# Seven block products for eight in the two dense layers of layer 3 of a graph network

## The chip, the cores and the metric

The kernel runs on one core of a Trainium2 chip. The metric is the device time of one execution in microseconds, as the median of several runs.

## The reference

32 graphs (B) of 512 nodes (N) with 256 features (D) pass through four layers. Each layer multiplies a full adjacency matrix with the features, passes the result through dense layers, adds the layer's input and normalizes each row (a layer norm over 256 features). All is f32.

```python
# x: (32, 512, 256), adj: (32, 512, 512)
x = ln(x + relu(((1 + eps0) * x + adj @ x) @ W1_0 + b1_0) @ W2_0 + b2_0)     # layer 0, hidden 512
h = adj @ (x @ W.T + b);  x = ln(x + where(h > 0, h, alpha * h))               # layer 1
h = ln(x) * gamma + beta
x = ln(x + x + relu(adj @ h @ W_rel + b_rel + h @ W_root))                     # layer 2
agg = eps3 * x + adj @ x                                                       # layer 3, hidden 1024
h = silu(rmsnorm(agg @ W1_3 + b1_3) * w_3)
x = ln(x + h @ W2_3 + b2_3)
```

## The kernel before

**One graph.** `adjT` holds the transposed adjacency matrix as four row blocks of 128 x 512 (8 KB a partition in all). The self loops are written into its diagonal blocks by GpSimd (POOL): `dg` saves the old diagonal, `loop0` and `loop3` are added for layers 0 and 3, and `rows` is the sum over the four blocks, whose column sums are needed in layers 1 and 2. `aggregate` multiplies `x` with `adjT` (four products of 512 columns into one PSUM bank, for each half j of the features), and ScalarE (ACT) copies the bank to `aT`, features on partitions. `dense_feat` keeps features on partitions (512 columns, two banks at a time), `dense_tok` gives tokens on partitions (256 columns). `Norm` computes a layer norm: VectorE (DVE) takes statistics of each block of 128 tokens (`half`), POOL takes the power -0.5 (`inv_sqrt`, tile `rstd`), DVE scales the four blocks (`scaled`).

**Layer 3**, where the change is, in `graph`: dense 1 is `dense_feat(aT, W1_3, f0)`, eight feature tiles of 128 x 512, two at a time. DVE adds the bias and writes `hT` (tile by tile), ACT squares the same bank (`acc`, `sq`), POOL adds the squares up in `acc`. `column_sums(acc)` (products with `ones`, one column each) gives the sum of squares of each token; DVE makes `ve` of it (L375), POOL the power, and four transposes against `ident` (L380) spread 1/rms over the partitions. DVE multiplies the eight tiles of `hT` with it (L385), ACT applies Silu (L386). Dense 2 is `dense_tok([(hT, W2_3)], h)` for two halves of the tokens, DVE adds `xb` (the layer's input and bias) into `r`, and the last `Norm` gives the output.

In layer 1 the product with W_1 is followed by a chain on DVE and ACT: `v`, `neg`, `s`, `r`, then a norm with two powers at once (128 x 8) that gives both the input of layer 2 (`h` in the change, `x` before) and a scaled copy (`xx`). `u` is the bias of layer 2, made from `rs` (the column sums of `rows`).

**The order.** Two graphs are under way at a time (STREAMS = 2): the generator `graph` yields after each piece of PE work, with a number of PE columns for which the stream is not to be resumed. Only PE's order is set by hand in this way: at each step the stream of the lowest graph number whose time has come goes on, and where none is due the count jumps ahead. `columns` counts what PE has been given, by a cost for each product. The order on DVE, ACT, POOL and the DMA queue comes from a scheduler at build time; each engine then takes its own queue strictly in that order.

```python
    WAIT_COPY, WAIT_NORM, WAIT_NORM2 = 2000, 11000, 17000
    WAIT_SQUARES, WAIT_RMS, WAIT_SILU = 6000, 5000, 8000
            columns[0] = max(columns[0], min(s[1] for s in live))
            s = min(s for s in live if s[1] <= columns[0])
```

**Buffers.** The pool `work` has two buffers for each name, shared by both streams (`v` and `neg` have one), `load` has three for `x` and `adjT`, PSUM eight banks. `prepare` loads a graph two graphs ahead; it is called in layer 3 (`successor`). Before the first graph, `fold_norm` multiplies gamma and beta of layer 2 into W_rel and W_root; these are PE's first products.

Of the kernel before, what the change touches and what calls it, by code (L numbers as in the profile page):

```python
# [12 lines left out]
P = 128  # L13
# [5 lines left out]
def tile_gnn_stack(ctx: ExitStack, tc: tile.TileContext, a: dict, out: bass.AP):  # L19
# [10 lines left out]

    nc = tc.nc
# [7 lines left out]
    HC = NC // 2  # L39

    const = ctx.enter_context(tc.tile_pool(name="const", bufs=1))
    load = ctx.enter_context(tc.tile_pool(name="load", bufs=3))
    work = ctx.enter_context(tc.tile_pool(name="work", bufs=2))
# [77 lines left out]
    def mm(o, lhsT, rhs, start, stop):  # L121
        nc.tensor.matmul(o, lhsT, rhs, start=start, stop=stop)  # L122
        columns[0] += 4 * max(o.shape[-1], P // 2)
# [15 lines left out]
    def tok(name, **kw):  # L139
        return work.tile([P, NC, D], F32, tag=name, name=name, **kw)  # L140

    def feat(name, n=DC, **kw):
        return work.tile([P, n, N], F32, tag=name, name=name, **kw)
# [40 lines left out]
    class Norm:  # L184
# [22 lines left out]
        def scaled(self, s, name):  # L207

            y = tok(name)
# [6 lines left out]

    def inv_sqrt(ve, name):
# [5 lines left out]
    def plus_row(x, r, name):  # L223

        y = tok(name)
        for h in range(2):
            nc.gpsimd.tensor_add(half(y, h), half(x, h), r.unsqueeze(1).to_broadcast([P, HC, D]))  # L227
        return y


    def load_graph(b):
        adjT = load.tile([P, NC, N], F32, tag="adjT", name="adjT")
# [5 lines left out]
    def prepare(b):  # L238

        x, adjT = load_graph(b)  # L240
        dg = work.tile([P, NC, P], F32, tag="dg", name="dg")
# [3 lines left out]
        rows = work.tile([P, N], F32, tag="rows", name="rows")  # L245
        nc.gpsimd.tensor_add(rows, adjT[:, 0, :], adjT[:, 1, :])
        for m in range(2, NC):
            nc.gpsimd.tensor_add(rows, rows, adjT[:, m, :])
        for m in range(NC):
            nc.gpsimd.tensor_add(loops[m], dg[:, m, :], loop0)  # L250
        return x, adjT, dg, rows, plus_row(x, b2_0, "xb")

    def graph(b, ready, successor):


        x, adjT, dg, rows, xb = ready
        loops = diagonal(adjT)


        aT = feat("aT")  # L260
# [5 lines left out]
        h1 = feat("h1", FC0)  # L266
# [5 lines left out]
        norm = Norm(tok("r"))  # L272
# [6 lines left out]
        x = norm.scaled(norm.scales((1.0, LN_EPS)), "x1")  # L279
# [3 lines left out]
        aT = feat("aT")  # L283
# [5 lines left out]
        u = tok("u")  # L289
        for c in range(NC):  # L290
            nc.vector.scalar_tensor_tensor(
                u[:, c, :], shift_rel, rs[:, c : c + 1], shift_2, op0=ALU.mult, op1=ALU.add
            )
        aggregate(aT, x, adjT, 1)
        yield WAIT_COPY
        v = tok("v", bufs=1)
        neg = tok("neg", bufs=1)
        s = tok("s")
        norm = Norm(tok("r"))
# [17 lines left out]
        h = norm.scaled(q[:, 0:NC], "x2")  # L317
# [153 lines left out]
```

## Time and profile before

| | |
|---|---|
| runs | 2737.19, 2737.64, 2738.63 us; median 2737.64 |
| profiled execution | 2741.19 us, of which the span of its instructions is 2739.3 |
| busy share of the span | PE 98%, PEld (weight loads) 60%, DVE 48%, POOL 35%, ACT 24% |
| granted TensorE clock, mean | 0.993 |
| DMA | 73.14 MB, mean 27 GB/s |

An f32 product that the code writes once is recorded as two PE instructions, a transpose as one. "f32 x1536" in a group is the number of recorded instructions. A line with an engine and "L122" is the helper `mm`, so products are told apart by the tiles' names: `ps<-aT,L_gnn_W` is a dense layer with features on partitions, `pst<-L_gnn_W,hT` is dense 2 of layer 3, `pst<-L_gnn_W,h` is W2_0 of layer 0, `pst<-L_gnn_W,aT` is W_1 of layer 1, `ps<-ones,acc` is the sum of squares, `ps<-ident,rstd` are the transposes of 1/rms. In a timeline a row has its start in us, its length, the engine, line and operation, its count and, in brackets, the idle time before it and who ended that. A row of windows has, after the stretch and its length, the busy time of each engine with its instructions, the granted clock, the DMA share and GB/s.

### The profile page before, as it was taken

What the parts mean: (1) busy time and instruction counts of PE and PEld (TensorE: products, weight loads), DVE (VectorE), ACT (ScalarE), POOL (GpSimd) and SP (SyncE); (2) the same over time, 40 slices, a digit from 0 to 9 for tenths busy, and PEclk for the clock granted to TensorE, in tenths of its full rate; (3) what the DMA queues carried; (4) which work ended last, traced back from release to release, by engine and by line L of the source; (5) the groups of instructions that cost most, each with busy time, mean ns of one, the idle gap of its engine ahead of it and who ended that gap; (6) DMA issues with size and microseconds to landing.
All of it is one profiled execution on the core that took longest, in us unless ns stands there. A gap on an engine that the chain in (4) does not pass through costs nothing.

```text
span 2739.3 us, 24444 instructions
## 1 busy us (share of the span) xinstructions
PE 2671.0 (98%) x9096; PEld 1651.8 (60%) x9096; DVE 1307.3 (48%) x3053; ACT 652.8 (24%) x1026; POOL 957.5 (35%) x1138
## 2 busy tenths in 40 slices
PE   6899999999999999999999999999999999999997
PEld 3556665666666666665666656666566666656664
DVE  2535544455454545535445444554545555444453
ACT  1222222212222122222222222222221222212221
POOL 4422434334333333433334343243433333333222
PEclk9999999999999999999999999999999999999998
DMA  4000000000000000000000000000000000000000
GB/s 150 16 31 16 24 31 24 31 16 31 31 16 31 31 22 25 16 31 31 31 16 24 31 24 31 16 24 31 24 31 16 31 31 16 31 24 8 8 8 8
DMA packets 17319, 73.14 MB, mean 27 GB/s; under 512 B 1969, under 2 KB 4273, under 8 KB 13105
## 3 DMA queue, kind: packets, MB, share of 16 engines
q1 hardware_dynamic: 13824, 67.12, 6.8%
q10 hardware_dynamic: 2928, 3.93, 0.4%
q8 instruction: 72, 1.18, 0.2%
q0 software_dynamic: 448, 0.54, 0.1%
q14 instruction: 47, 0.38, 0.0%
HBM read 54.80 MB, written 16.78 MB: 26 GB/s over the span
## 4 chain that ended last, share of the span: by engine, by line
PE 83%; POOL 8%; DVE 3%; issue 2%; ACT 2%; DMA 1%; POOLq 0%; ACTq 0%; DVEq 0%
PE ps L122 48%; PE pst L122 34%; POOL acc L371 7%; ACT sq L370 2%; PE ps L329 1%; DVE hT L365 1%; POOL rstd L220 1%; DMA L_gnn_W_rel<-in_L_gnn_W_rel_dram 1%; DVE st L194 1%; PE ps L380 1%; DVE r L343 0%; DVE s L342 0%; DVE x L211 0%; DVE mv L195 0%; DVE s L308 0%
## 5 line engine op out<-in xcount | busy, mean ns | idle before, releaser
L122 PE MATMUL ps<-adjT,x 128*128 128x512 f32 x2048 | 921.1, 598 | 19.3 <-DVE x L211 19.3
L122 PE MATMUL ps<-aT,L_gnn_W 128*128 128x512 f32 x1536 | 669.8, 592 | 0.0
L122 PEld LDWEIGHTS ps<-adjT,x 128*128 128x128 f32 x2048 | 385.0, 191 | 454.4 <-issue 411.5
L122 PEld LDWEIGHTS ps<-aT,L_gnn_W 128*128 128x128 f32 x1536 | 291.8, 190 | 367.4 <-issue 336.8
L153 ACT ACTIVATE aT<-ps 128x512 f32<-128x512 f32 x256 | 152.9, 597 | 1445.4 <-PE ps L122 1445.4
L122 PE MATMUL pst<-L_gnn_W,hT 128*128 128x256 f32 x2048 | 459.6, 384 | 3.1 <-ACT hT L386 3.1
L220 POOL TENSOR_TENSOR rstd<-ve,mhalf 128x4 f32<-128x4 f32 (+1 forms) x160 | 185.4, 1159 | 719.8 <-DVE ve L201 677.2
L122 PEld LDWEIGHTS pst<-L_gnn_W,hT 128*128 128x128 f32 x2048 | 387.2, 191 | 70.6 <-ACT hT L386 17.8
L371 POOL TENSOR_TENSOR acc<-acc,sq 128x512 f32<-128x512 f32 x224 | 283.3, 1265 | 368.5 <-ACT sq L370 360.8
L365 DVE TENSOR_SCALAR hT<-ps,L_gnn_b_c 128x512 f32<-128x512 f32 x256 | 192.2, 751 | 388.0 <-PE ps L122 374.2
L211 DVE TENSOR_SCALAR x<-r,mv,rstd 128x256 f32<-128x256 f32 x512 | 209.8, 473 | 189.8 <-POOL rstd L220 189.8
L122 PE MATMUL pst<-L_gnn_W,h 128*128 128x256 f32 x1024 | 232.4, 380 | 0.0
L227 POOL TENSOR_TENSOR xb<-x,L_gnn_b 128x512 f32<-128x512 f32 x128 | 163.4, 1292 | 165.7 <-DVE r L275 138.5
L122 PEld LDWEIGHTS pst<-L_gnn_W,h 128*128 128x128 f32 x1024 | 192.2, 190 | 31.7 <-issue 7.7
L370 ACT ACTIVATE sq<-ps,L_gnn_b_c 128x512 f32<-128x512 f32 x224 | 153.8, 687 | 205.2 <-DVE hT L365 108.4
L194 DVE BATCH_NORM_STATS2 st<-r 128x6 f32<-128x256 f32 x512 | 193.8, 415 | 5.5
L386 ACT ACTIVATE hT<-hT,L_gnn_rms_weight_c 128x512 f32<-128x512 f32 x256 | 162.7, 710 | 110.6 <-DVE hT L385 110.6
L385 DVE TENSOR_TENSOR hT<-hT,ps 128x512 f32<-128x512 f32 x256 | 157.4, 676 | 25.5 <-PE ps L380 25.5
L275 DVE TENSOR_TENSOR r<-pst,xb 128x512 f32<-128x512 f32 x64 | 43.9, 686 | 239.6 <-PE pst L122 239.6
L265 POOL COPY adjT<-dg 128x128 f32<-128x128 f32 x128 | 52.5, 410 | 273.7 <-PE ps L122 273.5
L342 DVE TENSOR_TENSOR s<-pst,u 128x512 f32<-128x512 f32 x64 | 44.3, 692 | 206.0 <-PE pst L122 206.0
L122 PE MATMUL pst<-L_gnn_W_root,h 128*128 128x256 f32 x512 | 131.4, 379 | 0.0
(65 smaller groups left out, 1768.0 us busy)
## 6 DMA issues: line engine op xcount, KB each, us to landing
adjT<-in_adj_dram SPq DMA_DIRECT2D x32, 1024.0 KB, 4.7
x<-in_x_dram SPq DMA_DIRECT2D x32, 512.0 KB, 3.4
out_dram<-x SPq DMA_DIRECT2D x32, 512.0 KB, 2.6
L_gnn_W<-in_L_gnn_W_dram ACTq DMA_DIRECT2D x2, 1024.0 KB, 14.8
L_gnn_W<-in_L_gnn_W_dram ACTq DMA_DIRECT2D x2, 512.0 KB, 12.5
L_gnn_b<-in_L_gnn_b_dram POOLq DMA_DIRECT2D x3, 128.0 KB, 8.2
L_gnn_W<-in_L_gnn_W_dram ACTq DMA_DIRECT2D x1, 256.0 KB, 19.9
L_gnn_W_rel<-in_L_gnn_W_rel_dram ACTq DMA_DIRECT2D x1, 256.0 KB, 20.1
```

What stands on the lines that cost most here:

```text
L122: nc.tensor.matmul(o, lhsT, rhs, start=start, stop=stop)
L153: nc.scalar.activation(aT[:, j, :], ps, AF.Copy)
L194: nc.vector.bn_stats(self.st[:, c, :], self.r[:, c, :])
L211: nc.vector.tensor_scalar(y[:, c, :], self.r[:, c, :], self.mv[:, c, 0:1], s[:, c : c + 1], op0=ALU.subtract, op1=ALU.mult,)
L220: nc.gpsimd.tensor_tensor(t, ve, mhalf[:, 0:n], op=ALU.pow)
L227: nc.gpsimd.tensor_add(half(y, h), half(x, h), r.unsqueeze(1).to_broadcast([P, HC, D]))
L265: nc.gpsimd.tensor_copy(loops[m], dg[:, m, :])
L365: nc.vector.tensor_scalar(hT[:, f, :], ps, bias, None, op0=ALU.add)
L370: nc.scalar.activation(sq, ps, AF.Square, bias=bias)
L371: nc.gpsimd.tensor_add(acc, acc, sq)
L385: nc.vector.tensor_mul(hT[:, f, :], hT[:, f, :], pr)
L386: nc.scalar.activation(hT[:, f, :], hT[:, f, :], AF.Silu, scale=w_3[:, f : f + 1])
```

## The change

Both dense layers of layer 3 are cut into 2 x 2 blocks on each side, and their product is formed by seven block products (Winograd's form of Strassen's method) where eight were needed. Four sums of blocks of each weight matrix are made once (`weight_sums`), four sums of blocks of the activations for each graph: dense 1 takes its sums of `aT` on DVE and POOL, dense 2 its sums of `hT` after the Silu, in part in place.

`seven` orders the products over three PSUM banks. Bank x takes m1, is read, and then goes on adding m6, m7 and m4, and is read after each; bank z takes m5, is read, and adds m3; bank y takes m2. So the partial sums of the method stay in PSUM. The first three reads (`take`) go to tiles `part`, the other four (`put`) make the blocks of the result. In dense 1 a product is two written matmuls of 256 columns (one step in K), and there are two rounds of seven; in dense 2 it is eight of 128 columns, one round. In dense 1 ACT now does the `take`s, half of the last `put` and the squares of two tiles at once, from SBUF; the last two additions to `acc` are on DVE.

Each stream has tiles of its own under a few names that several values share one after the other (`Slots`): `aT` and the norm's `r` share one, `x1`, `u` and the last `r` another, `h1`, `zT` and `hT` a third. `x` has two buffers for three. The sum `rows` moves from `prepare` into layer 0, `u` from layer 1 into layer 2, and the folding of gamma and beta into the first graph's layer 0. The cost per product in `mm` has another lower limit, WAIT_SQUARES is 9000 for 6000, and a WAIT_READ of 2000 stands ahead of m4.

```diff
+    TH = N // 2
+    STREAMS = 2
     const = ctx.enter_context(tc.tile_pool(name="const", bufs=1))
-    load = ctx.enter_context(tc.tile_pool(name="load", bufs=3))
-    work = ctx.enter_context(tc.tile_pool(name="work", bufs=2))
+    load = ctx.enter_context(tc.tile_pool(name="load", bufs=2))
+    work = ctx.enter_context(tc.tile_pool(name="work", bufs=1))
...
-    def mm(o, lhsT, rhs, start, stop):
-        nc.tensor.matmul(o, lhsT, rhs, start=start, stop=stop)
-        columns[0] += 4 * max(o.shape[-1], P // 2)
+    def mm(o, lhsT, rhs, start, stop, **kw):
+        nc.tensor.matmul(o, lhsT, rhs, start=start, stop=stop, **kw)
+        columns[0] += 4 * max(o.shape[-1], P + 4)
...
+        def tile(self, shape, tag, name):
+            return work.tile(shape, F32, tag=f"{tag}_{self.stream}", name=name)
...
+    def part():
+        return work.tile([P, 2, TH], F32, tag="part", name="part", bufs=6)
+    def scratch(name, **kw):
         return work.tile([P, NC, D], F32, tag=name, name=name, **kw)
...
+    def weight_sums(name, a11, a12, a21, a22):
+        t = const.tile([P, 4, *a11.shape[1:]], F32, tag=name, name=name)
+        s1, s2, s3, s4 = (t[:, i] for i in range(4))
+        nc.vector.tensor_add(s1, a21, a22)
+        nc.vector.tensor_sub(s2, s1, a11)
+        nc.vector.tensor_sub(s3, a11, a21)
+        nc.vector.tensor_sub(s4, a12, s2)
+        return dict(m1=a11, m2=a12, m3=s4, m4=a22, m5=s1, m6=s2, m7=s3)
...
+    def seven(product, quarter, take, put):
...
+        x, y, z = (psum.tile([P, *quarter], F32, tag="ps", name=n) for n in ("psx", "psy", "psz"))
+        product("m1", x, True)
+        t1 = take(x, 0, 0)
+        yield 0
+        product("m2", y, True)
+        put(y, t1, 0, 0)
+        product("m5", z, True)
+        t5 = take(z, 1, 1)
+        yield 0
+        product("m6", x, False)
+        t6 = take(x, 0, 1)
+        yield 0
+        product("m3", z, False)
+        put(z, t6, 0, 1)
+        yield 0
+        product("m7", x, False)
+        put(x, t5, 1, 1)
+        yield WAIT_READ
+        product("m4", x, False)
+        put(x, None, 1, 0)
...
     def load_graph(b):
-        adjT = load.tile([P, NC, N], F32, tag="adjT", name="adjT")
+        adjT = load.tile([P, NC, N], F32, tag="adjT", name="adjT", bufs=STREAMS + 1)
         x = load.tile([P, NC, D], F32, tag="x", name="x")
...
+        own = slots[b % STREAMS]
+        dg = own.tile([P, NC, P], "dg", "dg")
...
-        rows = work.tile([P, N], F32, tag="rows", name="rows")
-        nc.gpsimd.tensor_add(rows, adjT[:, 0, :], adjT[:, 1, :])
-        for m in range(2, NC):
-            nc.gpsimd.tensor_add(rows, rows, adjT[:, m, :])
         for m in range(NC):
             nc.gpsimd.tensor_add(loops[m], dg[:, m, :], loop0)
-        return x, adjT, dg, rows, plus_row(x, b2_0, "xb")
+        return x, adjT, dg, plus_row(own.tok("xb", "xb"), x, b2_0)
...
+        rows = own.tile([P, N], "rows", "rows")
+        nc.gpsimd.tensor_add(rows, adjT[:, 0, :], adjT[:, 1, :])
+        for m in range(2, NC):
+            nc.gpsimd.tensor_add(rows, rows, adjT[:, m, :])
+        h1 = own.feat("h", "h1", FC0)
...
-        norm = Norm(tok("r"))
+        if b == 0:
+            setup_weights()
+        norm = Norm(own.tok("aT", "r"))
...
-        u = tok("u")
-        for c in range(NC):
-            nc.vector.scalar_tensor_tensor(
-                u[:, c, :], shift_rel, rs[:, c : c + 1], shift_2, op0=ALU.mult, op1=ALU.add
-            )
...
-        v = tok("v", bufs=1)
-        neg = tok("neg", bufs=1)
-        s = tok("s")
-        norm = Norm(tok("r"))
+        v = scratch("v")
+        neg = scratch("neg")
+        s = scratch("s")
+        norm = Norm(own.tok("aT", "r"))
...
+        h = norm.scaled(q[:, 0:NC], own.tok("x2", "h"))
+        xx = norm.scaled(q[:, NC : 2 * NC], own.tok("xb", "xx"))
...
-        aT = feat("aT")
-        hT = feat("h1")
+        aT = own.feat("aT", "aT")
+        hT = own.feat("h", "zT")
+        u = own.tok("x1", "u")
+        for c in range(NC):
+            nc.vector.scalar_tensor_tensor(
+                u[:, c, :], shifts["rel"], rs[:, c : c + 1], shifts["2"], op0=ALU.mult, op1=ALU.add
+            )
...
-        t = tok("s")
-        norm = Norm(tok("r"))
+        t = scratch("s")
+        norm = Norm(own.tok("aT", "r"))
...
-        x = norm.scaled(norm.scales((1.0, LN_EPS)), "x1")
-        xb = plus_row(x, b2_3, "xb")
+        x = norm.scaled(norm.scales((1.0, LN_EPS)), own.tok("x1", "x1"))
+        xb = plus_row(own.tok("xb", "xb"), x, b2_3)
...
-        hT = feat("hT", FC3)
-        acc = work.tile([P, N], F32, tag="acc", name="acc")
-        for f0 in range(0, FC3, 2):
-            for i, ps in enumerate(dense_feat(aT, W1_3, f0)):
-                f = f0 + i
-                bias = b1_3[:, f : f + 1]
-                nc.vector.tensor_scalar(hT[:, f, :], ps, bias, None, op0=ALU.add)
-                if f == 0:
-                    nc.scalar.activation(acc, ps, AF.Square, bias=bias)
-                else:
-                    sq = work.tile([P, N], F32, tag="sq", name="sq", bufs=3)
-                    nc.scalar.activation(sq, ps, AF.Square, bias=bias)
-                    nc.gpsimd.tensor_add(acc, acc, sq)
-            yield WAIT_SQUARES if f0 + 2 == FC3 else 0
+        hT = own.feat("h", "hT", FC3)
+        acc = own.tile([P, N], "rows", "acc")
+        t = own.tile([P, 4, TH], "t", "t")
+        b11, b12, b21, b22 = (aT[:, k, j * TH : (j + 1) * TH] for k in range(2) for j in range(2))
+        t1, t2, t3, t4 = (t[:, i] for i in range(4))
+        nc.vector.tensor_sub(t1, b12, b11)
+        nc.vector.tensor_sub(t2, b22, t1)
+        nc.gpsimd.tensor_sub(t3, b22, b12)
+        nc.gpsimd.tensor_sub(t4, b21, t2)
+        right = dict(m1=b11, m2=b21, m3=b22, m4=t4, m5=t1, m6=t2, m7=t3)
+        FH = FC3 // 2
+        for f0 in range(0, FH, 2):
+            def product(m, ps, first):
+                for i in range(2):
+                    w = A1_3[m][:, (f0 + i) * P : (f0 + i + 1) * P]
+                    mm(ps[:, i, :], w, right[m], first and i == 0, True, skip_group_check=True)
+            def take(ps, i, j):
+                t = part()
+                nc.scalar.activation(t, ps, AF.Copy)
+                return t
+            def put(ps, t, i, j):
+                for n in range(2):
+                    f = i * FH + f0 + n
+                    o = hT[:, f, j * TH : (j + 1) * TH]
+                    bias = b1_3[:, f : f + 1]
+                    if t is None:
+                        nc.scalar.activation(o, ps[:, n, :], AF.Identity, bias=bias)
+                    else:
+                        nc.vector.scalar_tensor_tensor(
+                            o, ps[:, n, :], bias, t[:, n, :], op0=ALU.add, op1=ALU.add
+                        )
+                if i != j:
+                    f = i * FH + f0
+                    sq = work.tile([P, 2, N], F32, tag="sq", name="sq", bufs=2)
+                    nc.scalar.activation(sq, hT[:, f : f + 2, :], AF.Square)
+                    if f == 0:
+                        nc.gpsimd.tensor_add(acc, sq[:, 0, :], sq[:, 1, :])
+                    else:
+                        e = nc.vector if f + 2 == FC3 else nc.gpsimd
+                        e.tensor_add(acc, acc, sq[:, 0, :])
+                        e.tensor_add(acc, acc, sq[:, 1, :])
+            yield from seven(product, (2, TH), take, put)
+            yield WAIT_SQUARES if f0 + 2 == FH else 0
...
+        t1 = own.tile([P, FH, TH], "aT", "t1")
+        t2 = own.tile([P, FH, TH], "t", "t2")
+        b11, b12, b21, b22 = (
+            hT[:, k * FH : (k + 1) * FH, j * TH : (j + 1) * TH] for k in range(2) for j in range(2)
+        )
+        for q in (slice(0, FH // 2), slice(FH // 2, FH)):
+            nc.vector.tensor_sub(t1[:, q], b12[:, q], b11[:, q])
+        for q in (slice(0, FH // 2), slice(FH // 2, FH)):
+            nc.vector.tensor_sub(t2[:, q], b22[:, q], t1[:, q])
+            nc.gpsimd.tensor_sub(b12[:, q], b22[:, q], b12[:, q])
         yield WAIT_SILU
-        norm = Norm(tok("r"))
-        for h in range(2):
-            ps = dense_tok([(hT, W2_3)], h)
-            nc.vector.tensor_add(half(norm.r, h), ps, half(xb, h))
-            norm.half(h)
-            if h == 0:
-                yield 0
-        y = norm.scaled(norm.scales((1.0, LN_EPS)), "x2")
+        norm = Norm(own.tok("x1", "r"))
+        right = dict(m1=b11, m2=b21, m3=b22, m4=b21, m5=t1, m6=t2, m7=b12)
+        def product(m, ps, first):
+            for i in range(HC):
+                for k in range(FH):
+                    mm(
+                        ps[:, i, :], right[m][:, k, i * P : (i + 1) * P], A2_3[m][:, k, :],
+                        first and i == 0 and k == 0, k == FH - 1, skip_group_check=True,
+                    )
+            if m == "m2":
+                for q in (slice(0, FH // 2), slice(FH // 2, FH)):
+                    nc.gpsimd.tensor_sub(b21[:, q], b21[:, q], t2[:, q])
+        def block(t, i, j):
+            return t[:, j * HC : (j + 1) * HC, i * P : (i + 1) * P]
+        def take(ps, i, j):
+            t = part()[:, :, 0:P]
+            nc.vector.tensor_add(t, ps, block(xb, i, j))
+            return t
+        def put(ps, t, i, j):
+            nc.vector.tensor_add(block(norm.r, i, j), ps, block(xb, i, j) if t is None else t)
+            if i == 1:
+                norm.half(j)
+        yield from seven(product, (HC, P), take, put)
+        y = norm.scaled(norm.scales((1.0, LN_EPS)), own.tok("x2", "y"))
         nc.sync.dma_start(out[b].rearrange("(p c) d -> p c d", c=NC), y)
...
     WAIT_COPY, WAIT_NORM, WAIT_NORM2 = 2000, 11000, 17000
-    WAIT_SQUARES, WAIT_RMS, WAIT_SILU = 6000, 5000, 8000
-    STREAMS = 2
...
+    WAIT_SQUARES, WAIT_RMS, WAIT_SILU, WAIT_READ = 9000, 5000, 8000, 2000
...
+    def setup_weights():
+        shifts["rel"] = fold_norm(Wrel, "shift_rel")
+        shifts["2"] = fold_norm(Wroot, "shift_2")
+        nc.vector.tensor_add(shifts["2"], shifts["2"], b_2)
+        H = HID3 // 2
+        A1_3.update(
+            weight_sums("A1_3", *(W1_3[:, k, i * H : (i + 1) * H] for i in range(2) for k in range(2)))
+        )
+        F = FC3 // 2
+        A2_3.update(
+            weight_sums(
+                "A2_3",
+                *(W2_3[:, k * F : (k + 1) * F, i * P : (i + 1) * P] for i in range(2) for k in range(2)),
+            )
+        )
...
-    shift_rel = fold_norm(Wrel, "shift_rel")
-    shift_2 = fold_norm(Wroot, "shift_2")
-    nc.vector.tensor_add(shift_2, shift_2, b_2)
```

## The prediction

> **What bounds the kernel now.** I read the page first (engine shares), then PE's groups by form, then PE's timeline over the end of a graph, then the queues of DVE and POOL in the one place where PE stood still for long.
>
> ```profile
> span 2739.3 us, 24444 instructions
> ...
> PE 2671.0 (98%) x9096; PEld 1651.8 (60%) x9096; DVE 1307.3 (48%) x3053; ACT 652.8 (24%) x1026; POOL 957.5 (35%) x1138
> ```
>
> TensorE is the bound. An f32 product written once is recorded as two; a transpose once. A "mean ns" holds the pipeline's tail, so I price by start to start, from the timeline of one steady graph (start, length, idle before it in brackets):
>
> ```profile
> 2640.14 1.05 PE L122 MATMUL ps<-ones,acc 128*128 128x1 f32 x8
> 2641.05 1.03 PE L122 MATMUL ps<-ones,rows 128*128 128x1 f32 x8
> 2641.95 3.68 PE L122 MATMUL ps<-adjT,x 128*128 128x512 f32 x8
> 2645.46 0.60 PE L380 MATMUL ps<-ident,rstd 128*128 128x128 f32 x4
> 2645.90 3.70 PE L122 MATMUL pst<-L_gnn_W,aT 128*128 128x256 f32 x16
> 2649.44 13.98 PE L122 MATMUL pst<-L_gnn_W,hT 128*128 128x256 f32 x64
> 2663.25 3.60 PE L122 MATMUL ps<-adjT,x 128*128 128x512 f32 x8
> 2666.68 1.04 PE L329 MATMUL ps<-ident,x 128*128 128x128 f32 x8
> ```
>
> 256 columns: (2663.25-2649.44)/64 = 0.216 us. 512 columns: 3.43/8 = 0.429. One column, so nearly only a weight load: 0.112 (most common spacing). A 128-column transpose with its own weight load: 0.110. With the counts of the groups PE must issue 3584 x 0.429 + 4608 x 0.216 + 512 x 0.112 + 384 x 0.109 = 2632 us, plus 3 for the folded weights; about 104 us of the span is something else: 22.6 before the first product, some 24 at the end, 13 in the place below, the rest small.
>
> The reader should see what lies between `ones,acc` and `hT`: 4.3 us of the other graph's work covers the chain to 1/rms, and 3.5 us (`W,aT`) covers the Silu. In the first graph the cover is missing:
>
> ```profile
> 124.77 3.62 PE L122 MATMUL pst<-L_gnn_W,aT 128*128 128x256 f32 x16
> 129.14 1.05 PE L122 MATMUL ps<-ones,acc 128*128 128x1 f32 x8 [0.76 <-POOL acc L371]
> 137.39 1.12 PE L380 MATMUL ps<-ident,rstd 128*128 128x128 f32 x4 [7.19 <-POOL rstd L220]
> 140.04 16.63 PE L122 MATMUL pst<-L_gnn_W,hT 128*128 128x256 f32 x64 [1.54 <-ACT hT L386]
> ```
>
> The wait is not the chain's own length. DVE and POOL take their queues in order, and the other graph's norm (from `v`) stands in front of the rms step (`ve<-ps`) and of the multiplications of hT:
>
> ```profile
> 126.69 0.87 DVE L304 SCALAR_TENSOR_TENSOR v<-L_gnn_b,rs,pst 128x256 f32<-128x256 f32 x2 [0.97 <-PE pst L122]
> ...
> 134.39 0.15 DVE L375 TENSOR_SCALAR ve<-ps 128x4 f32<-128x4 f32 x1
> 136.24 1.38 DVE L211 TENSOR_SCALAR x<-r,mv,rstd 128x256 f32<-128x256 f32 x4 [1.70 <-POOL rstd L220]
> 138.54 3.08 DVE L385 TENSOR_TENSOR hT<-hT,ps 128x512 f32<-128x512 f32 x5 [0.92 <-PE ps L380]
> ```
>
> ```profile
> 134.56 2.78 POOL L220 TENSOR_TENSOR rstd<-ve,mhalf 128x8 f32<-128x8 f32 x2 [5.47 <-DVE ve L375]
> ```
>
> And the granted clock (last but two) falls to half around idle time or one-column products:
>
> ```profile
> 126.00:138.00 12.00, 4.05 (x23) 3.33 (x22) 8.46 (x23) 3.05 (x4) 5.71 (x5) 0.73 0.00 1
> 138.00:142.00 4.00, 2.46 (x8) 1.68 (x7) 3.46 (x6) 2.73 (x5) 0.00 (x0) 0.50 0.02 4
> ```
>
> ```profile
> 469.50:472.90 3.40, 3.40 (x6) 1.34 (x5) 2.43 (x4) 0.00 (x0) 3.40 (x3) 0.50 0.00 0
> ```
>
> The second stretch, in a later graph, follows `ones,acc` and `ones,rows` with no gap over 0.25 us: eight adjT products took 5.38 there, not 3.60.
>
> From the end of `W,aT` (128.23) to the end of dense 2 (156.45) this took 28.2 us where 15.2 were to issue: a loss of 13.0.
>
> **The change, part by part.** *Products.* Dense 1: 32 x 0.429 = 13.73 us becomes 7 x 4 written products, 56 x 0.216 = 12.10. Dense 2: 64 x 0.216 = 13.82 becomes 7 x 8, 112 of 128 columns. No row has a 128-column f32 product; below it lies the transpose (0.109), above it a load and a stream that don't overlap (0.112 + 0.107 = 0.219). I take 0.112, since the transposes show load and stream of that shape overlapped: 12.54. Saved 2.91 a graph, 93 in all. The Trainium skill (TensorE: Matmul & The Clock Gate, Back-to-back issue gap) speaks against small products: it gives 81 ns a product at 128 columns against 131 at 512. By that ratio, 0.62, a 128-column one would be an estimated 0.27 us and dense 2 30 us, which would add some 550 us; the transposes' row decides.
>
> *The order on PE.* In the built program's instruction order the due times have shifted the two graphs against each other. For the 15 even graphs from the third on, W_1's 16 recorded products (3.46) now stand before `ones,acc`; nothing stands between `ones,acc` and the transposes, and nothing between these and dense 2: the configuration of the first graph above. For 14 odd graphs, 16 of the other graph's W2_0 (3.46) stand before, nothing after `ones,acc`, and 3.44 us of adjT before dense 2.
>
> *Even windows.* Count from the end of dense 1's last product. ACT drains it (two halves, 0.8), squares 1024 elements (about 1.1, from 0.69 for 512), DVE adds twice: `ones,acc` starts at 4.0 instead of 3.46. DVE's queue, from `v` at 1.93: 4 v x 0.39, 2 acc adds x 0.60, 2 s x 0.67, 2 r x 0.60, 4 statistics x 0.33 with 0.4 of aggregates, 3 u x 0.40 (u has moved here), 0.2: `ve<-ps` at 10.4. (Without acc and u the trace took 7.7 for this, with one s at 1.38.) Then POOL's two powers, 3.0 as above: transposes at 13.4. DVE goes on with 4 h and 4 xx (8 x 0.32) before the eight multiplications, which start 4.45 after `ve<-ps` (0.2 to POOL, its first power 1.65, then 2.6), at 14.85; the first product follows 1.5 later (138.54 to 140.04): 16.35, where PE would be there at 4.8. So 11.5. Then the Silus arrive every 0.61, the second product needs the last of them, and the clock is halved: 1.8 to 3.8 more. I take 14.3, near the 13.0 measured; the ends are 11 (no pacing) and 17 (a slow s, all at half clock). 15 x 14.3 = 215.
>
> *Odd windows.* DVE: acc adds to 3.5, the other norm's r, statistics and `ve` to 5.4, `ve<-ps` 5.5; POOL 1.0 and 1.2; transposes at 7.75 instead of 4.36: 3.3. On ACT the copy of adjT's result stands before the fifth Silu and waits for PE, 1.0 more: 4.3. The four one-column pairs, 3.2 us of idle time and four transposes in a row are less work for PE than what stands ahead of 469.5, so I add that stretch's 5.38 - 3.60 = 1.8 nearly whole: 6.0 (3.5 to 8). 14 x 6.0 = 84. The skill's same page (Why this matters for your kernels) ties the loss of the full clock to idle gaps over about 3 us; by that alone the stretch at 469.5 would not have been halved, and the row above differs.
>
> *Other waits added.* r now lies in aT's slot, so its first half waits for the second half's products; the row sums moved into layer 0 put three POOL adds (1.27) in front of a power: x comes at about 7.5 where the filler ends at 6.9, once a pair. Before odd graphs' last norm, two POOL adds of xb (2.5) stand in front of the power; y's four scalings then hold up DVE for the other graph's h: 15.05 against 13.8. Together 2.2 a pair, 32 (0 to 60). In dense 1 the reads of a bank between its products are ACT copies of 0.60; with 0.2 to start and 0.05 to PE they fit into one product (0.864), but in the second round a square stands in front: 0.23 a graph, 7.
>
> *Waits that go.* The first graph's window now has 3.6 and 3.6 of filler: -13. The 0.97 before adjT in every pair (16 times): its filler after W_root grows from 3.5 to 6.9: -16. The 0.25 before `ones,acc`, and others that the windows swallow: -11. Sum -40.
>
> *Start.* PE begins with the folded weights at 22.57, when W_rel lands, and W1_0's products start at 32.81. Now adjT's come first; ACT can copy only from 22.4 (its queue issues weights until 20.7, then loads a table), W1_0 at about 24.2; the fold's 1.7 comes later: -7. The eight sums of weights (about 0.6 each) run on a DVE that waits until 46.8.
>
> *At nothing.* DVE gains some 6 us a graph of 41, ACT 4 of 20, POOL 4 of 30: throughput stays under PE's. x with two buffers: its slot is free from layer 0 on, its load lands in 3.4. The last graph runs alone: uncovered reads, above all those before the product m4 (1.2 twice), cost about what it saves.
>
> Sum: -93 + 215 + 84 + 32 + 7 - 40 - 7 = +198. The profiled execution took 2741.2, so 2939; the median of the runs is 3.6 below it: 2936.
>
> **Rivals.** (1) *Faster*: the windows are covered after all, as in 30 graphs before, where the same chain costs PE under 1 us. Then -93 - 7 + 39 and about -27 of waits gone: 2650. It decides when the 29 windows cost less than 101 / 29 = 3.5 us each. Against it stand the queue order and the first graph's 13.0. (2) Even windows pay, but odd ones keep the clock (-25) and the added waits mostly lie beside other work (-25): 2886. (3) Even windows are all at the upper end (+40), and DVE's reads in dense 2 queue behind the other graph, 32 x 0.4 more: 2990. (4) The product is not what it says: load and stream of 128 columns don't overlap, 112 x 0.107 more a graph, 383: near 3300.
>
> **How the numbers follow.** Forecast 0.58, (1) 0.10, (2) 0.18, (3) 0.12, (4) 0.02. The range, 2825 to 3005, takes even windows of 11 with odd ones of 3.5 and few added waits (-50 - 35 - 25) at one end and the upper ends of both windows (+40 + 28) at the other; it leaves out (1) and (4). A measurement of this kernel tells 0.2% from no change; faster is (1), 0.10, and 0.01 I leave for a tie.
>
> **What would show it.** Right: products of psx, psy, psz spaced 0.216 and 0.112; idle before the transposes put down to POOL's rstd, about 8 us in even graphs and 3 in odd ones; PEclk under 0.95; half-clock stretches in nearly every graph. Wrong: PE still at 97% or more, or no idle time before the transposes; or a spacing in dense 2 near 0.2.

## The result and the profile after

The changed kernel takes 3003.89 us, median of 4 runs (3001.80 to 3005.16); the kernel before, on the same chip, 2738.07. The ratio is 1.097, with a 95% interval of 1.0951 to 1.0989. The forecast was 2936, the range 2825 to 3005: the direction and the mechanism came as forecast, the size lies at the upper end of the range.

The head of the page of the changed kernel: span, busy shares, and the row of the granted clock over the 40 slices.

```profile
span 2999.9 us, 30408 instructions
...
PE 2683.3 (89%) x11400; PEld 1856.3 (62%) x11400; DVE 1444.1 (48%) x3605; ACT 775.6 (26%) x1218; POOL 1146.0 (38%) x1266
...
PEclk9999899999999999999999999999999999999998
```

PE is busy 89% of the span for 98%, and part of that at half clock (mean 0.951 for 0.993). The timeline of PE in an even graph, to be held against the first graph's window of the kernel before:

```profile
1038.87 1.03 PE L135 MATMUL psx<-t,L_gnn_W 128*128 128x256 f32 x4
1039.74 3.62 PE L135 MATMUL pst<-L_gnn_W,aT 128*128 128x256 f32 x16
1043.80 1.05 PE L135 MATMUL ps<-ones,acc 128*128 128x1 f32 x8 [0.44 <-DVE acc L466]
1053.28 1.12 PE L477 MATMUL ps<-ident,rstd 128*128 128x128 f32 x4 [8.43 <-POOL rstd L281]
1056.21 4.34 PE L135 MATMUL psx<-L_gnn_W,hT 128*128 128x128 f32 x16 [1.81 <-ACT hT L483]
1060.34 2.42 PE L135 MATMUL psy<-L_gnn_W,hT 128*128 128x128 f32 x16
```

`W,aT` (the other graph's W_1) stands before `ones,acc`, and then PE stands still for 8.43 and 1.81 us. The queue of DVE over the same time says why:

```profile
1041.67 0.48 DVE L363 SCALAR_TENSOR_TENSOR v<-L_gnn_b,rs,pst 128x256 f32<-128x256 f32 x1 [5.97 <-PE pst L135]
...
1049.54 0.45 DVE L385 SCALAR_TENSOR_TENSOR u<-shift_rel,rs,shift 128x256 f32<-128x256 f32 x1
1049.91 0.23 DVE L229 TENSOR_SCALAR ve<-mv 128x4 f32<-128x4 f32 x2
1050.05 0.15 DVE L472 TENSOR_SCALAR ve<-ps 128x4 f32<-128x4 f32 x1
1050.12 0.47 DVE L385 SCALAR_TENSOR_TENSOR u<-shift_rel,rs,shift 128x256 f32<-128x256 f32 x1
1052.13 1.38 DVE L238 TENSOR_SCALAR h<-r,mv,rstd 128x256 f32<-128x256 f32 x4 [1.54 <-POOL rstd L281]
1053.43 1.37 DVE L238 TENSOR_SCALAR xx<-r,mv,rstd 128x256 f32<-128x256 f32 x4
1054.72 3.66 DVE L482 TENSOR_TENSOR hT<-hT,ps 128x512 f32<-128x512 f32 x6
```

`ones,acc` is done at 1044.85, but `ve<-ps` waits its turn until 1050.05, 8.4 us after the other graph's norm began with `v`. The two powers on POOL follow, for both graphs in one row:

```profile
1050.21 3.01 POOL L281 TENSOR_TENSOR rstd<-ve,mhalf 128x8 f32<-128x8 f32 x2 [11.57 <-DVE ve L472]
```

Then come DVE's eight scalings to h and xx, which end at 1054.8, just after the transposes (1054.4); the multiplications of hT are next. The clock in and after this window (rows of windows, the granted clock last but two):

```profile
1047.70:1061.40 13.70, 6.31 (x26) 5.58 (x27) 12.16 (x32) 5.01 (x8) 4.06 (x3) 0.50 0.00 0
1061.40:1064.50 3.10, 3.10 (x30) 3.10 (x30) 1.34 (x3) 0.00 (x0) 3.10 (x3) 1.00 0.00 0
```

An odd graph, where adjT products are left as cover behind the transposes:

```profile
1128.47 1.05 PE L135 MATMUL ps<-ones,acc 128*128 128x1 f32 x8
1132.55 0.72 PE L477 MATMUL ps<-ident,rstd 128*128 128x128 f32 x4 [3.03 <-POOL rstd L281]
1133.06 5.27 PE L135 MATMUL ps<-adjT,x 128*128 128x512 f32 x8
1138.17 1.95 PE L135 MATMUL psx<-L_gnn_W,hT 128*128 128x128 f32 x16
```

5.27 us for eight adjT products that take 3.60 at full clock. PE's three largest waits (in us in total, times, longest); the first is the one before the transposes in both graphs shown, the other two lie elsewhere, at layer 2's input h and at x:

```profile
PE ps L477 <- POOL rstd L281: 170.4, 30, 8.4
PE ps L135 <- DVE h L238: 31.8, 30, 2.0
PE ps L135 <- DVE x L238: 31.8, 17, 5.5
```

For a ledger I take, from the trace, the distance of each PE instruction from the next and subtract its usual spacing (0.429, 0.216, 0.112 and 0.109 us for 512, 256 and 128 or 1 columns and transposes). What is left, the *loss*, is idle time and half clock together. "Issue" is the sum of the usual spacings. A *window* runs from dense 1's last product to the end of dense 2 (with seven products, of m2). The kernels below are those of the experiments.

| kernel | us | loss: 15 even windows | 14 odd | all else |
|---|---|---|---|---|
| before | 2738 | 9.6 | 12.1 | 51.1 |
| after | 3004 | 217.2 | 86.8 | 132.2 |
| e1 eight products, even windows uncovered | 2898 | 186.0 | 12.0 | 34.1 |
| e2 seven, order of before | 3009 | 8.6 | 20.9 | 405.4 |
| e3 seven, cover and reads | 2789 | 23.0 | 15.7 | 179.9 |
| e5 row sums and xb moved | 2973 | 223.7 | 93.4 | 84.9 |
| e7 no reads, cover | 2768 | 28.8 | 10.7 | 158.2 |
| e9 eight products, order of e7 | 2712 | 16.4 | 2.8 | 23.2 |
| e11 seven, all of it | 2669 | 36.1 | 10.7 | 55.0 |
| e12 POOL relieved | 2992 | 225.3 | 101.5 | 99.8 |

Issue is 2635.7 us with eight products and 2542.0 with seven. Before to after: -93.7 issue, +363.4 loss, -8.8 at the start (first product at 13.77 for 22.57): +260.9; the profiled executions, 2741.2 and 3001.8, differ by 260.6.

### The profile page after: what moved, and what is told of

Its sections match the earlier page's. It is cut to its first block, busy times and chain, and to the rows that moved or that the text cites. A ratio compares the mean times of both kernels' runs of the same rounds, so it can differ in the third digit from the quotient of the medians.

```text
span 2999.9 us, 30408 instructions
## 1 busy us (share of the span) xinstructions
PE 2683.3 (89%) x11400; PEld 1856.3 (62%) x11400; DVE 1444.1 (48%) x3605; ACT 775.6 (26%) x1218; POOL 1146.0 (38%) x1266
## 5 line engine op out<-in xcount | busy, mean ns | idle before, releaser
L135 PE MATMUL ps<-adjT,x 128*128 128x512 f32 x1536 | 712.3, 613 | 45.5 <-DVE x L238 31.8
L135 PE MATMUL ps<-adjT,h 128*128 128x512 f32 x512 | 242.1, 612 | 31.8 <-DVE h L238 31.8
L135 PE MATMUL ps<-aT,L_gnn_W 128*128 128x512 f32 x512 | 229.8, 592 | 1.0 <-ACT aT L181 1.0
L493 POOL TENSOR_TENSOR hT<-hT 128x512 f32<-128x512 f32 x64 | 119.3, 1885 | 239.8 <-DVE t L490 123.0
L135 PEld LDWEIGHTS psx<-L_gnn_W,hT 128*128 128x128 f32 x1024 | 152.7, 224 | 63.1 <-ACT hT L483 35.4
L135 PE MATMUL psx<-L_gnn_W,hT 128*128 128x128 f32 x1024 | 163.2, 322 | 29.4 <-ACT hT L483 28.7
L135 PEld LDWEIGHTS ps<-adjT,h 128*128 128x128 f32 x512 | 93.5, 194 | 144.9 <-issue 82.6
L238 DVE TENSOR_SCALAR x<-r,mv,rstd 128x256 f32<-128x256 f32 x256 | 121.2, 536 | 108.3 <-POOL rstd L281 108.3
L135 PEld LDWEIGHTS ps<-aT,L_gnn_W 128*128 128x128 f32 x512 | 97.2, 190 | 117.4 <-issue 107.1
L460 ACT ACTIVATE sq<-hT 128x1024 f32<-128x1024 f32 x128 | 135.3, 1057 | 89.7 <-DVE hT L454 86.1
L454 DVE SCALAR_TENSOR_TENSOR hT<-psy,L_gnn_b_c,part 128x256 f32<-128x256 f32 x128 | 56.1, 479 | 205.9 <-ACT part L443 179.7
```

The lines of the kernel that those rows point to most:

```text
L135: nc.tensor.matmul(o, lhsT, rhs, start=start, stop=stop, **kw)
L238: nc.vector.tensor_scalar(y[:, c, :], self.r[:, c, :], self.mv[:, c, 0:1], s[:, c : c + 1], op0=ALU.subtract, op1=ALU.mult,)
L454: nc.vector.scalar_tensor_tensor(o, ps[:, n, :], bias, t[:, n, :], op0=ALU.add, op1=ALU.add)
L460: nc.scalar.activation(sq, hT[:, f : f + 2, :], AF.Square)
L493: nc.gpsimd.tensor_sub(b12[:, q], b22[:, q], b12[:, q])
```

## Experiments

Theory: the order of PE's queue left the chain of 1/rms and Silu without the other graph's work beside it, and DVE's queue made that chain long. Rival: the seven products, their sums and the shared tiles cost by themselves.

**e1_even_uncovered.** Eight products, the old buffers, one number:

```diff
-    WAIT_COPY, WAIT_NORM, WAIT_NORM2 = 2000, 11000, 17000
+    WAIT_COPY, WAIT_NORM, WAIT_NORM2 = 2000, 11000, 27000
```

> The kernel before, eight products and its old buffers, with WAIT_NORM2 at 27000 for 17000. In its PE order this puts the 16 W_1 products before `ones,acc` in the even graphs from the third on, and nothing between `ones,acc`, the transposes and dense 2; the odd graphs keep their cover (3.5 and 3.5 us). Theory (the uncovered window is the cost, whatever the products): 15 windows of 13 to 14.5 us, so 195 to 217 us more than 2738, 2930 to 2955. Rival (the seven products or the shared slots are the cost): no such windows without them, 2738 with at most 30 us either way. A third case: the window is costly only with u and the last two adds to acc on DVE, then some 10 us each, 2890.

Measured: 2898.31, ratio 1.0584 (1.0568 to 1.0599). An even graph on PE:

```profile
1020.07 1.05 PE L122 MATMUL ps<-ones,acc 128*128 128x1 f32 x8 [0.84 <-POOL acc L371]
1028.31 1.12 PE L380 MATMUL ps<-ident,rstd 128*128 128x128 f32 x4 [7.19 <-POOL rstd L220]
1030.96 15.58 PE L122 MATMUL pst<-L_gnn_W,hT 128*128 128x256 f32 x64 [1.53 <-ACT hT L386]
```

The order alone costs +159: windows +176 (12.4 each for 0.6), while x after layer 2 no longer waits (-15). That is 12.4 against 14.5 in the changed kernel: the wait before the transposes is 7.19 for 8.43, which fits that u and the adds to acc do not stand in this kernel's DVE queue there. The time comes nearest the expectation's third case, with 12.4 a window for its 10. So even windows cost without any of the seven products.

**e2_order_of_before.** Seven products, PE's cover as in the kernel before:

```diff
-    WAIT_SQUARES, WAIT_RMS, WAIT_SILU, WAIT_READ = 9000, 5000, 8000, 2000
+    WAIT_SQUARES, WAIT_RMS, WAIT_SILU, WAIT_READ = 6000, 5000, 8000, 0
```

> The changed kernel with WAIT_READ 0 for 2000 and WAIT_SQUARES 6000 for 9000: PE's order gets the cover of the kernel before again (4.3 and 3.5 us after `ones,acc` in even graphs, 3.5 and 3.5 in odd ones), the products stay seven. Theory (order): the 304 us of the 29 windows fall to 15 to 60; in exchange the three reads ahead of m4 have nothing beside them, 0.7 to 1.3 us each, 31 x 3.1 = 96, and x after layer 2 has 3.5 us of filler in the even graphs for 6.9, up to 48 more: 2800 to 2890. Rival (seven products and own tiles cost by themselves): above 2960.

Measured: 3008.60, 1.0991 (1.0958 to 1.1024). The windows went as the theory said (304 to 30 us), and the time did not fall at all: on the number, the rival was right. PE's waits in this kernel, and the place in an even graph where most of it is lost:

```profile
PE psx L135 <- DVE part L514: 88.3, 44, 3.8
PE ps L135 <- DVE x L238: 68.4, 32, 5.5
PE psx L135 <- DVE hT L454: 65.0, 64, 1.1
PE psx L135 <- DVE r L518: 27.7, 32, 1.2
```

```profile
1429.98 1.95 PE L135 MATMUL psz<-A,t 128*128 128x128 f32 x16
1435.68 3.78 PE L135 MATMUL psx<-A,t 128*128 128x128 f32 x16 [3.76 <-DVE part L514]
1439.71 2.94 PE L135 MATMUL psz<-A,hT 128*128 128x128 f32 x16 [0.25 <-DVE part L514]
```

m6 may not go on in bank x before DVE has read m1 from it, and that read stands in DVE's queue behind the sums for m6 and the other graph's `v` and `s`:

```profile
1428.96 3.43 DVE L492 TENSOR_TENSOR t<-hT,t 128x512 f32<-128x512 f32 x2
1432.32 1.64 DVE L363 SCALAR_TENSOR_TENSOR v<-L_gnn_b,rs,pst 128x256 f32<-128x256 f32 x4
1433.88 1.41 DVE L367 SCALAR_TENSOR_TENSOR s<-neg,nalpha,x 128x512 f32<-128x512 f32 x1
1435.22 0.41 DVE L514 TENSOR_TENSOR part<-psx,xb 128x256 f32<-128x256 f32 x1
```

The reads ahead of m4 (L454, L518) cost about 1 us each, three a graph. So the changed kernel spent the other graph's work on the reads (WAIT_READ) and had none for the windows; e2 does the opposite and loses as much. e2 changes two numbers at once. Following the due times through the code with its own cost per product (worked out, not run) tells them apart: with WAIT_SQUARES alone at 6000 the order of a pair stays that of the changed kernel, with WAIT_READ alone at 0 the transposes have cover ahead of them again, and in odd graphs behind them too.

**e3_cover_and_reads.** Seven products, an order with cover for both:

```diff
-    WAIT_COPY, WAIT_NORM, WAIT_NORM2 = 2000, 11000, 17000
-    WAIT_SQUARES, WAIT_RMS, WAIT_SILU, WAIT_READ = 9000, 5000, 8000, 2000
+    WAIT_COPY, WAIT_NORM, WAIT_NORM2 = 2000, 16000, 31500
+    WAIT_SQUARES, WAIT_RMS, WAIT_SILU, WAIT_READ = 4000, 5000, 5000, 2000
```

> The changed kernel with four numbers of its order changed: WAIT_NORM 16000 for 11000, WAIT_NORM2 31500 for 17000, WAIT_SQUARES 4000 for 9000, WAIT_SILU 5000 for 8000. Both windows have 3.4 to 3.6 us of the other graph's work on each side, and m4 of the second round and of dense 2 keep work ahead of them. Theory (order): the windows fall from 304 to some 40 us, the waits outside (117) stay at 80 to 130, with about 20 new before m4 of the first round: 2700 to 2790. Rival (seven products and own tiles cost by themselves): above 2960.

Measured: 2788.62, 1.0183 (1.0168 to 1.0198). Four numbers take back 215 us of the 266, inside the theory's range. Of what is left outside the windows, about 55 us stand before m6 of dense 1's first round, whose sum `t` (L429) waits in DVE's queue behind h and xx.

**e4_idle_products.** Unused products in the changed kernel's windows:

```diff
         yield WAIT_RMS
+        if 1 < b < B - 1:
+            idle_products(6 if b % 2 else 18)
...
         yield WAIT_SILU
+        if 1 < b < B - 1:
+            idle_products(3 if b % 2 else 5)
```

> The changed kernel with products that are not used put into the windows on PE (even graphs: 18 written ones of 256 columns after `ones,acc`, 5 after the transposes; odd ones: 6 and 3); nothing waits for them. Theory (clock): they lie in idle time and keep the clock up, so the products of dense 2 and the adjT products behind them run at full speed: 2 us less an even window, 1 an odd one, and 25 us of half-clock products outside: 3004 - 30 - 14 - 25 = 2935 (2925 to 2965), with PEclk near 1 in the windows. Rival (the Silus and the reads pace dense 2, the clock only follows): 3000 to 3010. If they delay what comes behind them: up to 3040.

Measured: 2993.81, 1.0933 (1.0915 to 1.0951): 10 us, not 69. With the unused products' own 203.5 us counted as idle time, the even windows lost 13 us less and the odd ones 19 less; dense 2's first two products still lose 1.92 an even window for 2.79, which fits the pace of the Silus. Behind the odd graphs' waits for h the adjT products ran at half clock more often than before (31.4 us for 12.7). The clock is the smaller part of a window, and keeping it up in one place moved part of the loss to another; why there, stays open.

**e5_rows_xb_moved.** POOL's row sums back in `prepare`, layer 2's xb adds later:

```diff
-        xb = plus_row(own.tok("xb", "xb"), x, b2_3)
         yield WAIT_NORM
...
+        xb = plus_row(own.tok("xb", "xb"), x, b2_3)
         successor()
```

> The changed kernel with the row sums back in `prepare` (a tile of their own) and layer 2's xb adds issued after the two adjT products of layer 3; PE's order is that of the changed kernel. Theory (POOL's queue): the waits of adjT for h in the odd graphs (15 times, 30.0 us in all) and for x after layer 2 (14 times, 24.8) come from POOL work in front of a power and go, with some of the half-clock adjT products (12.7) that follow them: 2935 to 2965. Rival (DVE's queue or PE's order makes them): 2995 to 3010.

Measured: 2972.55, 1.0852 (1.0833 to 1.0871), 8 us above the expectation's upper end. In the trace the wait of x is gone (24.8 to 0), that of h halved (30.0 to 15.9), the half-clock products behind it fell from 12.7 to 3.3; against that the windows grew by 13, and the start by 5.3 (the row sums now stand before the first product). So POOL's row sums made the wait of x and half of that of h, in two ways. For x they stood in front of the power: in the changed kernel DVE's `ve` is done at 908.9 and the power starts at 911.93, behind the row sums. For h the power waited for DVE, and DVE was slow, with a `u` of 1.39 us beside a row sum on POOL. Three rows of the changed kernel, and the same `u` in e5:

```profile
982.58 1.58 POOL L327 TENSOR_TENSOR rows<-rows,adjT 128x512 f32<-128x512 f32 x1
983.05 1.39 DVE L385 SCALAR_TENSOR_TENSOR u<-shift_rel,rs,shift 128x256 f32<-128x256 f32 x1
984.67 1.81 POOL L281 TENSOR_TENSOR rstd<-ve,mhalf 128x8 f32<-128x8 f32 x1 [0.51 <-DVE ve L229]
```

```profile
979.19 0.45 DVE L385 SCALAR_TENSOR_TENSOR u<-shift_rel,rs,shift 128x256 f32<-128x256 f32 x1
```

The 0.94 between the two is what the wait of h lost (2.09 to 1.14 in each odd graph). The other half stays in e5, where two xb adds still stand in front of the last norm's power (967.99 to 970.44).

**e6_no_reads_old_order, e7_no_reads_cover.** Dense 1's rounds side by side, m4 of dense 2 in a bank of its own, e5's edits; e6 with e2's order of the windows, e7 with another:

```diff
+        for n, r in enumerate((ra, ra, rb, ra, rb, ra, rb, ra, rb, ra, rb, ra, rb, rb)):
+            next(r)
...
-    WAIT_COPY, WAIT_NORM, WAIT_NORM2 = 2000, 11000, 17000
-    WAIT_SQUARES, WAIT_RMS, WAIT_SILU = 6000, 5000, 8000
+    WAIT_COPY, WAIT_NORM, WAIT_NORM2 = 2000, 13500, 21000
+    WAIT_SQUARES, WAIT_RMS, WAIT_SILU = 12500, 5000, 7500
```

> Seven products, PE's order as in the kernel before, as in e2_order_of_before, but with the reads and operand sums out of PE's way: the two rounds of dense 1 run side by side on six banks, so that two or three products lie between two uses of a bank; POOL makes the sums of aT; dense 2 orders its products m1, m2, m5, m6, m3, m7, m4, with m4 in a bank of its own and its operand in the free tile t1; row sums and xb as in e5_rows_xb_moved. Theory (the loss of e2 is the reads ahead of m6 and m4 and the sums they need, about 250 us with the half-clock products behind): 2700 to 2780. Rival (those waits only stand in for others that come next on DVE and POOL): above 2880.

> As e6_no_reads_old_order, with WAIT_NORM 13500, WAIT_NORM2 21000, WAIT_SQUARES 12500, WAIT_SILU 7500: the filler is 6.9 to 7.7 us before `ones,acc` and 3.4 to 3.6 on each side of the transposes in both graphs of a pair. Theory (cover decides): windows under 1.5 us each, little left outside, 2640 to 2710, faster than the kernel before. Rival (the work added on DVE, ACT and POOL now sets the pace): no lower than e6_no_reads_old_order.

Measured: e6 2986.94, 1.0904 (1.0885 to 1.0923), on the rival's side: the reads ahead of m4 shrank, but m1's read still stood in DVE's queue (psx waits for `part` 88.0 us, as in e2), and `ones,acc` came to wait for the squares. e7 2767.94, 1.0114 (1.0083 to 1.0145): lower than e6 by 219, but above the 2640 to 2710 expected. Spacing the products out did little where DVE was behind anyway; the order did much.

**e8_m4_own_bank, e9_before_same_order.** e8: e7 with m4 of dense 1 in bank y (and the two smaller moves that its expectation names). e9: the kernel before with e7's four numbers.

```diff
-            product("m4", x, False)
-            put(x, None, 1, 0)
+            product("m4", y, True)
+            put(y, t7, 1, 0)
```

> As e7_no_reads_cover, with m4 of dense 1 written to bank y (free since m2 was read) instead of going on in bank x, so that it waits for no read just issued; m7's sum is read once by ACT, and DVE adds it to m4. The subtraction for m7's operand in dense 2 stands on DVE behind the sums for m6, and the row sums of the first two graphs are made in layer 0 again. Theory (what was left were reads ahead of m4, 55 and 39 us, the products at half clock behind them, 12, the sum for m6, 11, and 5 at the start): 2640 to 2690, below the kernel before. Rival (DVE, now with four more adds a graph, queues the same waits elsewhere): 2740 to 2790.

> The kernel before, eight products, with the four numbers of e7_no_reads_cover (WAIT_NORM 13500, WAIT_NORM2 21000, WAIT_SQUARES 12500, WAIT_SILU 7500). It tells how much of a gain is the order and not the seven products. Theory (products): the kernel before has only some 50 us of waits in its steady part, so 2700 to 2740, and the rest of the difference to e8_m4_own_bank is the 93 us of products less what their sums and reads still cost. Rival (order alone): as fast as e8_m4_own_bank.

Measured: e8 2753.68, 1.0046 (1.0028 to 1.0064); e9 2711.71, 0.9900 (0.9885 to 0.9914). In e8 the waits before m4 (55.1 us in e7's first round and 39.1 in its second) fall to about 6, and `ones,acc` waits instead. The first row is PE's wait, the second that of DVE's last adds to acc:

```profile
PE ps L135 <- DVE acc L448: 59.9, 32, 7.7
DVE acc L447 <- POOL acc L448: 143.6, 32, 4.7
```

The rival's number is met, but through POOL's adds and not through a late DVE. e9 is faster than the kernel before by 1.0%: the order had 27 us to give there too, inside its theory's range. In the same order seven products (e7) are 56 us slower than eight (e9): 94 less to issue, some 155 more of waits. The trace of e8 shows one source of such waits, DVE and then POOL in the same stretch:

```profile
1465.98 2.75 DVE L238 TENSOR_SCALAR h<-r,mv,rstd 128x256 f32<-128x256 f32 x4 [1.54 <-POOL rstd L257]
1468.65 4.43 DVE L238 TENSOR_SCALAR xx<-r,mv,rstd 128x256 f32<-128x256 f32 x4
```

```profile
1468.97 1.27 POOL L276 TENSOR_TENSOR rows<-adjT 128x512 f32<-128x512 f32 x1 [0.71 <-DMA adjT<-in_adj_dram]
1470.32 2.62 POOL L278 TENSOR_TENSOR rows<-rows,adjT 128x512 f32<-128x512 f32 x2
```

Four scalings that took 1.37 in the changed kernel above take 4.43 while POOL adds.

**e10_squares_on_dve, e11_rows_on_dve.** POOL's adds to DVE, one group after the other:

```diff
-                        e = nc.vector if f + 2 == FC3 else nc.gpsimd
+                        e = nc.vector
...
-        nc.gpsimd.tensor_add(rows, adjT[:, 0, :], adjT[:, 1, :])
+        nc.vector.tensor_add(rows, adjT[:, 0, :], adjT[:, 1, :])
```

> As e8_m4_own_bank, with six of the seven adds into acc on DVE (0.60 us each in the trace) for five of seven on POOL (1.27 each). In e8_m4_own_bank the reads were gone, and `ones,acc` waited 2.7 us in even graphs and 1.1 in odd ones for this row of adds, with products at half clock behind it. Theory (POOL's adds are the last of the chain): 1.2 to 2.7 us less an even graph, 1.1 an odd one, and 1.7 of half-clock products: 2690 to 2720. Rival (the last square on ACT, or a DVE that is now late, ends the chain at the same time): 2740 to 2760.

> As e10_squares_on_dve, with the three adds of the row sums on DVE for POOL too. In e8_m4_own_bank DVE's scalings of h and xx took 0.8 to 1.4 us each for 0.40 while POOL made these adds. Theory (DVE and POOL hold each other up when both run): DVE gains about 4 us before the puts of dense 1 in the even graphs and spends 1.8 on the adds; 10 to 30 us less than e10_squares_on_dve. Rival (three more adds in DVE's queue delay what stands behind them, contention costs nothing on the path): no lower than e10_squares_on_dve.

Measured: e10 2696.61, 0.9835 (0.9813 to 0.9857); e11 2668.76, 0.9738 (0.9722 to 0.9755), both as the theories said. From e10 to e11 the 128 scalings to xx fell from 728 to 404 ns on average, while POOL's powers waited for DVE in 144 of 160 cases in both, which speaks for DVE coming free and not for POOL's queue. e11 beats the kernel before by 2.6% and e9, the eight products in that order, by 43 us. Of the 43, 8 are the earlier start (first product at 15.58 for 23.60), and the rest is 94 of issue less 59 of loss. Eight products with that start and with POOL's adds on DVE were not run; to come as low as e11, e9 would then have to shed 35 of its 42.4 us of loss.

The page of e11:

```profile
span 2667.3 us, 30426 instructions
...
PE 2587.2 (97%) x11400; PEld 1819.2 (68%) x11400; DVE 1635.3 (61%) x4021; ACT 747.1 (28%) x1154; POOL 761.7 (29%) x1010
```

**e12_pool_relieved.** The same relief of POOL in the changed kernel, with PE's order left as it is (row sums, acc, and):

```diff
-            nc.gpsimd.tensor_sub(b12[:, q], b22[:, q], b12[:, q])
+            nc.vector.tensor_sub(b12[:, q], b22[:, q], b12[:, q])
```

> The changed kernel with POOL's row sums, its adds into acc but the first, and its subtraction for m7's operand in dense 2 on DVE, in their places; PE's order, and so the windows, as in the changed kernel. Theory (PE's order makes the windows, POOL only the waits outside and some slow DVE operations): the 14 waits of x after layer 2 (24.8 us) go, those for h (30.0) stay or halve, the 29 windows stay at 280 to 305 us in all: 2945 to 2980. Rival (contention of DVE and POOL made the windows too, as it did in e10 and e11): below 2900. If DVE's longer queue lengthens the windows: above 3000.

Measured: 2992.42, 1.0917 (1.0898 to 1.0935), between the cases. Outside the windows 32 us went, the windows grew by 23; the even window's wait before the transposes stayed at 8.60. Taking POOL's work over to DVE doesn't shorten the windows; it was worth 11 us here, 57 and 28 once the order was mended (e10, e11).

## Why the prediction was right, and where it was too small

*Products.* 128-column products are spaced 0.112, 256-column ones 0.216: -93.7 us, as summed. The ratio of 0.62 that the prediction weighed from the Trainium skill (TensorE: Matmul & The Clock Gate, Back-to-back issue gap), an estimated 0.27 us, is not borne out here.

*Even windows.* 14.48 each, 217 in all, for 14.3 and 215, and by the same parts: 0.6 to `ones,acc`, 8.6 to the transposes, 2.5 to the first product, 2.8 of Silus and clock. e1 shows the order as a sufficient cause; that the queue of DVE sets the length is read from the trace's order and from e1's window, shorter by u and acc; no run reorders DVE alone.

*Odd windows.* 6.20 each, 87 in all, for 6.0 and 84: 3.2 before the transposes, 1.8 for adjT at half clock, 0.9 for the late Silus.

*Start.* -8.8 for -7. *First graph's window* -10 for -13; *the 0.97 before adjT in every pair* -13.9 for -16. The mean clock, 0.951, just missed the sign "PEclk under 0.95".

*What failed* is the step "other waits added", with the terms of its kind. The windows net of what the kernel before lost there were forecast at 215 + 84 - 13 - 11 = 275 and came to 318.7 - 45.7 = 273. Outside them the prediction had +32 + 7 - 16 = +23; measured 27.0 to 117.5, +90.5. The waits of h and x, priced at 32, cost 30.0 + 24.8 = 54.8: 2.0 an odd graph's h for 1.3, 1.8 an x for 0.6 (whose shares, 1.3 and 0.6, make 1.9 a pair and not the 2.2 of the sum). Of h, the part that was forecast, xb in front of a power, fits the 1.14 that e5 leaves (the power starts 1.2 after its input there, behind xb); the 0.94 of a `u` held up beside POOL had no term. The adjT products behind h run at half clock, 12.7 that had no term. Small waits inside dense 1 cost 17.5 for 7. Three waits of PE before m4 cost 11.1 where nothing stood: 1.2 and 1.1 are the last graph's, as priced, and 8.7 is the first graph's second round, whose read of bank x stands in DVE's queue behind the other graph's h and xx:

```profile
128.32 2.07 PE L135 MATMUL psx<-t,L_gnn_W 128*128 128x256 f32 x4 [8.57 <-DVE hT L454]
```

So most of what the first graph's window gained was lost just ahead of it. With 2 on the -16 these make 59 of the 67 us; the rest is scattered. Windows, start and products give back some 4, so the profiled executions are 63 above the forecast's sum. The medians are 68 above it, because the forecast's last step took the median to lie 3.6 below the profiled execution, as in the kernel before, and here it lies 2.1 above.

*Luck.* The mechanism and the windows were foreseen, but that 3004 lies inside a range that ends at 3005 is luck: that end was made of longer windows (+40 and +28), the windows came as forecast, and the excess came from other terms.

*The rivals.* Covered windows with seven products (rival 1, 2650) were made in e2: covered, and 3009. Its sum took the reads in seven for 7 us, since WAIT_READ hid those before m4; without that cover the waits for bank x alone took 181 us (88.3 + 65.0 + 27.7), with half-clock products and later waits behind them. Only e11, with the reads, POOL's adds and the order all changed, comes near that number. DVE's dense 2 reads behind the other graph (half of rival 3) did not show in the changed kernel, but are what e2 lost most by.

## What to carry to other kernels

Work of another stream that covers a wait is a budget: a new yield that hides a 1 us read with 3.5 us of work takes that cover from a longer chain, so count what each wait needs before and after, for the whole period of the order, and print the order. Saving 3.5% of the bound engine's products is worth something only if the sums and reads that it adds on other engines stay off the path; price them with the cover gone. And compare against the old kernel in the new order: e9 shows that the order was worth 27 us without any of the new products.

## What the runs showed of the hardware

- DVE scalings of 128x256 took 1.42 us for 0.40 while POOL added 128x512 tiles (e8), and DVE's subtractions of 128x512 1.7 for 0.68 while POOL subtracted (e2, 3.43 for two). In e8 POOL's adds stayed at 1.27, and a DVE scaling that started with a POOL operation lasted about 0.15 longer than it (0.88 beside 0.73, 1.42 beside 1.27); in e2 POOL was slow too, 1.56 to 1.71 a subtraction for 1.26. Taking POOL's row sums away was worth 28 us (e10 to e11). The Trainium skill (SBUF — State Buffer, SBUF: two separate sides) states that DVE and GpSimd share a pair of ports under an exclusive lock; the runs agree that the two hold each other up; in e8 only DVE was held up.
- In the even window shown, the granted clock fell to half and came back 13.7 us later, with PE busy for 6.3 of that time; in the odd one it was at half for 3.4 us. Unused products in the idle time kept it up there and lost it elsewhere (e4).
